# First attention of a gated cross-attention kernel: an own PSUM tile for greatest scores, sums of two key tiles together, small products for both token tiles, shorter roots, and a new opening

## The chip, the cores and the metric

The kernel runs on one core of a Trainium2 chip. The metric is the device time of one execution in microseconds. One execution was also profiled; durations, waits and the clock granted to TensorE come from it. PE is TensorE's matmul, PEld its weight load, DVE is VectorE, ACT is ScalarE, POOL is GpSimd, SP is SyncE, which issues most DMAs.

## The reference, cut to what matters

Two layers, each of cross attention and a feed-forward part, on 4 batches of 256 tokens of width 256 and a context of 1601 tokens of width 128. The change lies in the cross attention of the first layer alone:

```python
y_dca = y[:, -DCA:, :]          # the last 16 context tokens
y_main = y[:, :-DCA, :]         # 1585 others
k_dca = _ln(kv_dca[:, :, 0], kn_dca_w, kn_dca_b)
q = _ln((x @ Wq + bq).reshape(b, s1, H, HD), qn_w, qn_b)
kv = jnp.concatenate([y_main @ Wk + bk, y_main @ Wv + bv], axis=-1)
kv = kv.reshape(b, s2, H, 2 * HD)
k = _ln(kv[..., :HD], kn_w, kn_b)          # per head of 16
v = kv[..., HD:]
ctx = _attn(qT, k.transpose(0, 2, 1, 3), v.transpose(0, 2, 1, 3))
ctx_dca = _attn(qT, k_dca..., v_dca...)    # a softmax of its own
return (ctx + DCA_WEIGHT * ctx_dca) @ Wo + bo
```

There are 16 heads of width 16; all is fp32. x is layer-normed before, and the result is added to x times the tanh of a gate.

## The kernel before

**Tiling.** The stage handles slabs: a slab is four heads of one batch, so there are 4 x 4 = 16. A head occupies 32 partitions (its width of 16, shared between two slabs), so a product with keys uses 32 rows of the array, and two heads run beside each other in two of its four row groups. The 1585 keys are 13 key tiles of 128, taken in seven pairs, the last a single one. A slab has 14 slots: seven pairs times two halves of its heads.

**A slot.** Each slot emits, in this order:

- A, `attend_tile` (L723 to L742): scores of two heads for two key tiles, four products of 256 columns on 32 rows (L732) into a PSUM tile of two banks, and later their exponential on ACT into `e` (L742).
- G, `greatest_tile` (L676 to L703): for the slab after this one, scores the other way round, two products of 453 columns (L688) into a PSUM tile of two banks, and their maximum on DVE (L697, or L699 for the last columns of both token tiles). The maxima of a slab, 14 G tiles, give its shift (`shift`, L708).
- W, `weigh` (L748 to L766): the sums over one key tile of exponentials times values, four products in four column groups (L757), added up in `ps_o` over the slab.
- What the plan has put into the slot.

The heart of it, and the pools of PSUM tiles:

```python
ps_s = ph.enter_context(tc.tile_pool(name="l0ps_s", bufs=3, space=PSUM))
ps_o = ph.enter_context(tc.tile_pool(name="l0ps_o", bufs=1, space=PSUM))
ps_m = ph.enter_context(tc.tile_pool(name="l0ps_m", bufs=1, space=PSUM))
...
exponentials = attend_tile(u, k)
if ahead:
    v, _ = ahead.pop(0)
    next_greatest(v, 2 - TILES[k][2])
exponentials()
t = k - 2
if t >= 0:
    weigh(u, t)
elif t == -2 and u > 0:
    weigh(u - 1, NKT - 1)
for step in plan.pop(u * SLOTS + k, []):
    step()
```

A and G take turns in the three tiles of `ps_s`. The order on each engine is the order of emission (`keep_order`).

**The plan.** `place` puts a step into a slot; `book` puts one that needs the single tile of `ps_m` (a small product) into the first slot that has none. Small products are: turns of queries (L664), heads into the token layout (`add_heads`, L779), turned heads and output projection per token tile (L795, L803), layer norms (L130), query projections (L551), key products (L472), root sums (L502), values (L535), the last tokens' attention in four products per token tile (L588, L596, L618, L626), and routing for the later part (L202, L241). The scaling of keys (`key_scale`, L525 and L527) takes a tile of `ps_s`. Batch b + 1 is prepared while batch b is attended.

**Roots.** A key's variance per head comes from a product of its squares with `hsum` (L502), 16 heads and one column for the unscaled last rows on 32 partitions, for four groups of 397 keys; then a logarithm, an exponential and a Newton step on 128 x 397 (L509 to L516), and a product with `sel` that spreads the roots over the heads' rows (L525).

**The opening.** Before the first slot the kernel loads weights and the first context, prepares batch 0 (keys, queries, roots, values), the 16 last keys of all batches (`prepare_last`, L402), makes the 14 G tiles of slab 0 and the first four (`LEAD`) of slab 1.

Of the kernel before, what the change touches and what calls it, by code (L numbers as in the profile page):

```python
# [21 lines left out]
P = 128  # L22
# [10 lines left out]
H = 16  # L33
# [26 lines left out]
def tile_gated_cross_blocks(ctx: ExitStack, tc: tile.TileContext, a: dict, out: bass.AP):  # L60
# [49 lines left out]
    def layernorm_steps(b, pst, tag="ps_t"):  # L110
# [15 lines left out]
        yield  # L126
        for i, xn in enumerate(xns):
            pt = pst.tile([P, 512], F32, name=tag)
            for c in range(DC):
                nc.tensor.transpose(pt[:, c * P : (c + 1) * P], xn[:, c * P : (c + 1) * P], ident)  # L130
            nc.scalar.copy(
                xnT[b][:, :, i * P : (i + 1) * P],
                pt[:, : DC * P].rearrange("p (c t) -> p c t", c=DC),
            )
            yield
# [126 lines left out]
    KG = (NMAIN + NG - 1) // NG  # L262
# [4 lines left out]
    with ExitStack() as ph:  # L267
# [7 lines left out]
        ps_s = ph.enter_context(tc.tile_pool(name="l0ps_s", bufs=3, space=PSUM))  # L275
# [17 lines left out]
        wkv = wp.tile([P, 2 * D], F32, name="wkv")  # L293
# [3 lines left out]
        for i, n in enumerate(("L0_xattn_bk", "L0_xattn_bv")):  # L297
# [9 lines left out]
        hn = {  # L307
            n: bcast_row(wp, f"L0_xattn_{n}", HD0, nc.sync if "dca" in n else nc.scalar)
            for n in ("qn_w", "qn_b", "kn_b", "kn_w", "kn_dca_w", "kn_dca_b")
        }  # L310
        NB = B * DCA
        cd = lp.tile([P, NB], F32, name="cd")
        nc.sync.dma_start(out=cd.rearrange("p (b k) -> p b k", b=B), in_=a["ctxT"][:, :, NMAIN:])
        wdca = load(lp, "wdca", [P, 2 * D], a["Wkv_dca"])
        bdca = bcast_row(lp, "bkv_dca", 2 * D)
        bkv = lp.tile([NB, 2 * D], F32, name="bkv")
        for i, n in enumerate(("L0_xattn_bk", "L0_xattn_bv")):
            nc.sync.dma_start(out=bkv[:, i * D : (i + 1) * D], in_=a[n].partition_broadcast(NB))
        load_gates()
        for t in range(QT, 2 * QT):  # L320
            load_x(t)
        for g in range(NG):
            load_context(1, g)
        wo = load(wp, "wo0", [P, DC, D], a["L0_xattn_Wo"].rearrange("(c p) n -> p c n", p=P))
        bo = bcast_row(wp, "L0_xattn_bo", D)
        for t in range(2 * QT, NT):
            load_x(t)
# [6 lines left out]
        epsc = wp.tile([P, 1], F32, name="epsc")  # L334
        hsum = wp.tile([P, 2, W], F32, name="hsum")
        hsel = wp.tile([P, 2, NG, W], F32, name="hsel")
        sel = wp.tile([P, 2, P], F32, name="sel0")
# [14 lines left out]
        for c in range(2):  # L352
            nc.gpsimd.tensor_scalar(hsum[:, c, c * HW : (c + 1) * HW], bmask, 1.0 / HD0, None, ALU.mult)
# [3 lines left out]
        for c in range(2):  # L357
            nc.gpsimd.tensor_copy(hsel[:, c, :, c * HW : (c + 1) * HW], bc_mid(last_row, NG))
            nc.gpsimd.tensor_copy(hsel[:, c, :, H], m15.to_broadcast([P, NG]))
# [17 lines left out]
        w4, b4 = (x.rearrange("p (c h e) -> p c h e", c=2, e=2 * HD0) for x in (wkv, brow))  # L377
# [24 lines left out]
        def prepare_last():  # L402

            rep = lp.tile([NB, B, HG, DCA], F32, name="rep", bufs=1)
# [6 lines left out]
            kd = lp.tile([P, H, HD0], F32, name="kd", bufs=1)  # L411
            vd = lp.tile([P, H, HD0], F32, name="vd", bufs=1)
            ph3, bd3, bm3 = (x.rearrange("p (h e) -> p h e", e=2 * HD0) for x in (pm[:NB], bdca[:NB], bkv))
            nc.vector.tensor_tensor(kd[:NB], ph3[:, :, :HD0], bd3[:, :, :HD0], ALU.add)
            nc.vector.tensor_tensor(vd[:NB], ph3[:, :, HD0:], bd3[:, :, HD0:], ALU.add)

            nc.gpsimd.tensor_tensor(vd[:NB], vd[:NB], bm3[:, :, HD0:], ALU.add)
            yield
            center(kd[:NB], kd[:NB])
            sqd = lp.tile([P, H, HD0], F32, name="sqd", bufs=1)  # L420
            nc.scalar.activation(sqd[:NB], kd[:NB], AF.Square)
            yield
            v, y, t = (lp.tile([NB, H], F32, name=f"d_{k}", bufs=1) for k in "vyt")
            nc.vector.reduce_sum(v, sqd[:NB], axis=AX.X)
# [4 lines left out]
            nc.gpsimd.tensor_tensor(kd[:NB], kd[:NB], bc_last(v, HD0), ALU.mult)  # L429
            nc.gpsimd.tensor_tensor(kd[:NB], kd[:NB], bc_mid(hn["kn_dca_w"][:NB], H), ALU.mult)  # L430
            nc.gpsimd.tensor_tensor(kd[:NB], kd[:NB], bc_mid(hn["kn_dca_b"][:NB], H), ALU.add)
            yield
            pt = ps_m.tile([P, 512], F32, name="ps_m")
            for c in range(DC):
                nc.tensor.transpose(
                    pt[:, c * NB : (c + 1) * NB],
                    kd[:NB, c * HG : (c + 1) * HG, :].rearrange("p h d -> p (h d)"),
                    ident[:NB, :NB],
                )
            kdT = lp.tile([P, DC, NB], F32, name="kdT", bufs=1)  # L440
# [7 lines left out]
            for b in range(0, B, 2):  # L448
                pv = ps_m.tile([P, 512], F32, name="ps_m")
                for k in range(2):  # L450
# [3 lines left out]
                        rhs=vd[:NB].rearrange("p h d -> p (h d)"),  # L454
                        start=True,
                        stop=True,
                    )
                for k in range(2):
                    for c in range(DC):
                        nc.vector.tensor_tensor(  # L460
                            vdb[b + k][:, c],
                            pv[:, k * D + c * P : k * D + (c + 1) * P].rearrange("p (h d) -> p h d", d=HD0),
                            bc_last(bmask, HD0),
                            ALU.mult,
                        )
                yield

# [27 lines left out]
        def key_roots(b):  # L495

            v, y, t = (hp.tile([P, KG], F32, name=f"r_{k}") for k in "vyt")
            roots[b] = v
            pm = ps_m.tile([P, 512], F32, name="ps_m")
            for c in range(2):  # L500
                for g in range(NG):
                    nc.tensor.matmul(  # L502
                        pm[g * W : (g + 1) * W, :KG],
                        lhsT=hsum[:, c],
                        rhs=sq[:, c, g * KG : (g + 1) * KG],
                        start=c == 0,
                        stop=c == 1,
                    )
            nc.vector.tensor_scalar(v, pm[:, :KG], epsc, None, ALU.add)  # L509
# [9 lines left out]
        def key_scale(b, c, half):  # L519

            ps = ps_s.tile([P, 2, 512], F32, name="ps_s")
            for i in range(2):
                g = 2 * half + i
                rows = slice(g * W, (g + 1) * W)
                nc.tensor.matmul(ps[:, i, :KG], lhsT=sel[rows, c], rhs=roots[b][rows], start=True, stop=True)  # L525
            k3 = kTs[b % 2][:, c, 2 * half * KG : 2 * (half + 1) * KG].rearrange("p (i k) -> p i k", i=2)
            nc.vector.tensor_tensor(k3, k3, ps[:, :, :KG], ALU.mult)  # L527
# [18 lines left out]
        aos = [[fix.tile([P, D], F32, name=f"ao{j}{i}") for i in range(QT)] for j in range(2)]  # L546

        def query_project(b, i):
            pm = ps_m.tile([P, 512], F32, name="ps_m")
            for c in range(DC):  # L550
                nc.tensor.matmul(  # L551
                    pm[:, :D], lhsT=xnT[b][:, c, i * P : (i + 1) * P], rhs=wq[:, c, :], start=c == 0, stop=c == DC - 1
                )
            nc.vector.tensor_tensor(qraw[:, i].rearrange("p h d -> p (h d)"), pm[:, :D], bq, ALU.add)

        def query_steps(b, eng):
# [18 lines left out]

            eng.tensor_tensor(sqq, q3, bc_mid(hn["kn_b"], QT * H), ALU.mult)
            yield
            nc.vector.reduce_sum(qcs[b % 2].rearrange("p i h -> p (i h)"), sqq, axis=AX.X)
            eng.tensor_tensor(kb, q3, bc_mid(hn["kn_w"], QT * H), ALU.mult)
            yield  # L580

        def last_tokens(b):

            qn = qraw
# [1071 lines left out]
```

## Time and profile before

| | us |
|---|---|
| median of three runs | 1623.56 (1615.42 to 1623.99) |
| the profiled execution: its own time | 1621.13 |
| its span, first to last instruction | 1619.4 |
| opening of the stage, to the first A | 77.1 |
| the 224 slots | 500.3 |
| later stages | 1042 |

The rows of the profile name engine, line and operation, then what it writes from what it reads. A busy PE includes waits between its row groups, so PE's share of 97% does not say that the array is full. In a timeline row the first number is the start, the second the length; what stands in brackets is the idle time of the engine before it and what ended it. In the rows by stretches of time, busy time and number of instructions stand by engine, then the granted clock, the share of the DMA engines and the traffic.

### The profile page before, as it was taken

The page shows a single profiled execution, that of the slowest core. Times are in us where ns is not written, and L with a number is a line of the kernel's source. Part 1 is how long each engine was busy: PE and PEld are TensorE (multiplying, and loading weights), DVE is VectorE, ACT ScalarE, POOL GpSimd, SP SyncE. Part 2 cuts the span into 40 slices and gives each one's busy share as a digit, 9 for nine tenths or more (in the row PEclk, how much of TensorE's full clock was granted, in tenths as well). Part 3 has the DMA queues.
Part 4 walks back from the last instruction along what each step waited for, and adds up shares of the span by engine and source line. Part 5 has one row for each costly group of instructions (what it writes and reads, how often), then busy time and mean ns, then how long its engine had stood idle before and what let it go on. Part 6 is the DMA issues. An engine that isn't in the chain of part 4 may idle for free.

```text
span 1619.4 us, 31284 instructions
## 1 busy us (share of the span) xinstructions
PE 1566.6 (97%) x12200; PEld 915.5 (57%) x12200; DVE 1100.0 (68%) x2409; ACT 795.3 (49%) x1837; POOL 514.2 (32%) x424
## 2 busy tenths in 40 slices
PE   4899999999999999989999999999999999999998
PEld 2454544554555545446666666666666666666665
DVE  5566576566567436677777777777877778777655
ACT  2256556556555534444445454554445444454443
POOL 1101001001001124434445444454444444444410
PEclk8689999999999999989999999999999999999999
DMA  4000000000010040000000000000000000000000
GB/s 123 21 1 1 21 1 1 1 2 10 1 49 15 14 179 1 1 2 8 9 15 15 15 9 16 8 22 3 15 9 15 21 9 15 9 2 2 2 1 27
DMA packets 44713, 28.06 MB, mean 17 GB/s; under 512 B 29586, under 2 KB 40212, under 8 KB 44436
## 3 DMA queue, kind: packets, MB, share of 16 engines
q1 hardware_dynamic: 30852, 24.82, 5.3%
q10 hardware_dynamic: 13712, 1.23, 0.6%
q8 instruction: 96, 1.57, 0.4%
q14 instruction: 53, 0.43, 0.1%
HBM read 24.18 MB, written 1.05 MB: 16 GB/s over the span
## 4 chain that ended last, share of the span: by engine, by line
PE 88%; DVE 4%; ACT 3%; issue 3%; POOL 1%; DMA 1%; ACTq 0%; SPq 0%; DVEq 0%; POOLq 0%
PE ps_o L1433 21%; PE ps_sc L1370 20%; PE ps_s L732 9%; PE ps_o L757 7%; PE ps_s L688 7%; PE ps_y L1451 4%; PE ps_m L1359 3%; PE ps_v L1193 2%; PE ps_m L535 2%; PE ps_m L472 1%; ACT pr L1385 1%; PE ps_a L1207 1%; PE ps_m L664 1%; DVE mxs L697 1%; PE ps_g L1564 1%
## 5 line engine op out<-in xcount | busy, mean ns | idle before, releaser
L1420 POOL TENSOR_TENSOR pr<-pr,rs 128x1604 f32<-128x1604 f32 x128 | 364.0, 2865 | 432.4 <-DMA rs<-ws 386.2
L1433 PE MATMUL ps_o<-pT,cx 128*128 128x256 f32 x1664 | 372.5, 381 | 8.3 <-DVE pT L1426 8.3
L1370 PE MATMUL ps_sc<-ctxT,qT 128*32 128x401 f32 x4096 | 359.5, 502 | 0.5 <-DVE nm L1377 0.5
L1377 DVE CUSTOM_DVE_ANT_0 pr<-ps_sc,mk 128x401 f32<-128x401 f32 x512 | 294.1, 576 | 93.7 <-PE ps_sc L1370 55.3
L1385 ACT ACTIVATE pr<-pr,nm 128x401 f32<-128x401 f32 x512 | 320.8, 628 | 70.1 <-DVE nm L1377 69.6
L1433 PEld LDWEIGHTS ps_o<-pT,cx 128*128 128x128 f32 x1664 | 317.9, 191 | 53.1 <-DVE pT L1426 9.4
L697 DVE TENSOR_REDUCE mxs<-ps_s 128x2 f32<-128x906 f32 x192 | 210.4, 1100 | 139.7 <-PE ps_s L732 70.0
L742 ACT ACTIVATE e<-ps_s 128x1024 f32<-128x1024 f32 (+1 forms) x224 | 215.2, 963 | 174.8 <-PE ps_s L732 156.3
L1426 DVE STREAM_TRANSPOSE pT<-pr 128x1664 f32<-128x1664 f32 x128 | 242.9, 1899 | 4.9 <-POOL pr L1420 4.9
L1370 PEld LDWEIGHTS ps_sc<-ctxT,qT 128*32 128x32 f32 x4096 | 126.3, 110 | 204.3 <-issue 119.7
L732 PE MATMUL ps_s<-qT,kT 32*128 32x256 f32 x1664 | 240.1, 405 | 1.0 <-ACT e L742 0.9
L688 PE MATMUL ps_s<-kT,qT 32*128 32x453 f32 (+1 forms) x1024 | 232.3, 563 | 2.1 <-ACT e L742 1.2
L732 PEld LDWEIGHTS ps_s<-qT,kT 32*128 32x128 f32 x1664 | 142.2, 186 | 73.1 <-issue 39.7
L757 PE MATMUL ps_o<-e,vp 128*32 128x256 f32 x1664 | 134.3, 392 | 0.6 <-ACT e L742 0.6
L1402 ACT ACTIVATE ws<-ws 32x32 f32<-32x32 f32 x64 | 14.6, 228 | 194.1 <-DVE ws L1401 194.1
L1443 ACT COPY ao<-ps_o 128x256 f32<-128x256 f32 x64 | 23.8, 372 | 153.5 <-PE ps_o L1433 130.2
L1385 ACT ACTIVATION_READ_ACCUMULATOR pr<-pr,nm 128x1 f32 x512 | 95.5, 187 | 0.0
L688 PEld LDWEIGHTS ps_s<-kT,qT 32*128 32x128 f32 x1024 | 80.1, 192 | 11.7 <-issue 3.8
L757 PEld LDWEIGHTS ps_o<-e,vp 128*32 128x32 f32 x1664 | 33.2, 108 | 91.0 <-issue 88.5
L788 POOL TENSOR_TENSOR ao<-ao,on 128x64 f32<-128x64 f32 x32 | 10.4, 326 | 228.5 <-DVE rs L783 168.2
L1451 PE MATMUL ps_y<-vo,ao 128*128 128x256 f32 x256 | 72.3, 405 | 0.1
L1451 PEld LDWEIGHTS ps_y<-vo,ao 128*128 128x128 f32 x256 | 43.3, 189 | 44.5 <-ACT pr L1385 39.9
(291 smaller groups left out, 1505.8 us busy)
## 6 DMA issues: line engine op xcount, KB each, us to landing
ctxT<-in_ctxT_dram SPq DMA_DIRECT2D x4, 800.5 KB, 10.8
ctx<-in_ctxT_dram SPq DMA_DIRECT2D x12, 198.5 KB, 3.5
kT<-in_L_xattn_Wq_dram SPq DMA_DIRECT2D x4, 512.0 KB, 3.6
wo<-in_L_xattn_Wo_dram SPq DMA_DIRECT2D x4, 512.0 KB, 5.4
bq<-nm SPq DMA_DIRECT2D x128, 2.0 KB, 1.7
bq<-nm ACTq DMA_DIRECT2D x128, 2.0 KB, 2.0
rs<-ws SPq DMA_DIRECT2D x128, 1.0 KB, 1.9
rs<-ws ACTq DMA_DIRECT2D x128, 1.0 KB, 1.7
```

Source lines behind the costliest of these rows:

```text
L688: nc.tensor.matmul(ps[:, k, m * w : (m + 1) * w], lhsT=qT[rows, ii * P : (ii + 1) * P], rhs=kT[rows, s // 2, n * CW0 : n * CW0 + w], start ...
L697: nc.vector.tensor_reduce(mx[:, i, r : r + 2, n], ps[:, :, :w], AX.X, ALU.max)
L732: nc.tensor.matmul(ps[:, k, jj * S : (jj + 1) * S], lhsT=kT[rows, s // 2, (j + jj) * P : (j + jj + 1) * P], rhs=qT[rows], start=True, stop ...
L742: nc.scalar.activation(e[:, :, : nj * S], ps[:, :, : nj * S], AF.Exp)
L757: nc.tensor.matmul(summed[u][(r + k) * W : (r + k + 1) * W, :S], lhsT=vps[b % 2][:, t, h * VW : h * VW + W], rhs=made[u, j, r][:, k, jj * ...
L1370: nc.tensor.matmul(ps[i * TQ : (i + 1) * TQ, :KS], lhsT=queries[u][:, t * TQ : (t + 1) * TQ], rhs=ctxT[b][:, i * KS : (i + 1) * KS], start ...
L1377: nc.vector.tensor_tensor_reduce(out=prs[u % 3][:, t, :KS], in0=ps[:, :KS], in1=masks[b], scale=-1.0, scalar=3.0e38, op0=ALU.add, op1=ALU. ...
L1385: nc.scalar.activation(p, p, AF.Exp, bias=found[u][:, 0, t : t + 1], scale=-1.0, accum_out=found[u][:, 1, t : t + 1])
L1420: nc.gpsimd.tensor_tensor(p, p, bc_last(factors[:, ts], KS), ALU.mult)
L1426: nc.vector.transpose(pTs[u % 2][:, ts].rearrange("p t k -> p (t k)"), prs[u % 3][:, ts].rearrange("p t k -> p (t k)"))
L1433: nc.tensor.matmul(po[:, u % 2], lhsT=contexts[b][:, k, :], rhs=pTs[u % 2].rearrange("p t (k q) -> p t k q", q=TQ)[:, :, k, :], start=k == ...
L1451: nc.tensor.matmul(ys[b][:, i], lhsT=outs[u][:, i * P : (i + 1) * P], rhs=vo[:, h, :], start=(h, i) == (0, 0), stop=(h, i) == (H - 1, QT - 1),
```

## The change

- **PSUM.** `ps_s` has two tiles instead of three and is A's; a new pool `ps_g` with one tile is G's. In the opening, where there is no A, G and the first keys rotate over all three.
- **W.** In even slots W handles the two key tiles whose A tiles were made in the two slots before, together; in odd slots there is none. Slot 0 of a slab holds the last key tile of the slab before, alone.
- **Small products** for both token tiles in one group: transposes of tokens, query projection, the last tokens' four products, turned heads, output projection. `book` uses odd slots only; keys, values, roots and the last tokens may use any.
- **Roots** on 128 x 199: each group of 397 keys is halved, the halves lie in the two halves of the 32 partitions; root sums and spreading take twice as many products of half the columns. The unscaled row is added in `key_scale` by DVE (`m15`) instead of by a column of `sel`.
- **Opening.** `prepare_last` and the last tokens of batch 0 move into the first slots; slab 1's first four G tiles move into slots 1, 2, 5 and 6 of slab 0 (`CATCH_UP`). Most loads are issued after the first weights are centred (`load_rest`); the second key weights share the tile of the first (`w_first`). Three values are made while the roots are computed. The copies of `prepare_last` go to ACT and its arithmetic, with the output's gating, to POOL.

```diff
-        ps_s = ph.enter_context(tc.tile_pool(name="l0ps_s", bufs=3, space=PSUM))
+        ps_s = ph.enter_context(tc.tile_pool(name="l0ps_s", bufs=2, space=PSUM))
+        ps_g = ph.enter_context(tc.tile_pool(name="l0ps_g", bufs=1, space=PSUM))
...
-        def greatest_tile(u, n, i, r):
+        def greatest_tile(u, n, i, r, pool=None):
...
-            ps = ps_s.tile([P, 2, 512], F32, name="ps_s")
+            ps = (pool or ps_g).tile([P, 2, 512], F32, name="ps_g" if pool is None else "ps_s")
...
-        def book(slot, step):
+        def book(slot, step, any_slot=False):
...
-            while slot in taken:
+            while slot in taken or not (any_slot or slot % 2):
                 slot += 1
...
+        CATCH_UP = {1: 2, 2: 0, 5: 2, 6: 0}
...
-        for k in range(HALF_SLAB):
-            next_greatest(0, 0)
-            next_greatest(0, 2)
-            value_project(0, next(values))
-            next(last0, None)
...
+        for k in range(2 * HALF_SLAB):
+            next_greatest(0, k % 2 * 2, (ps_s, ps_s, None)[k % 3])
+            if k == 3:
+                for _ in qs0:
+                    pass
+            if k % 3 == 2:
+                value_project(0, next(values))
...
         turn_queries(0, 1)
-        turn_queries(1, 0)
-        for k in range(LEAD):
-            next_greatest(1, (2, 0)[k % 2])
-        for _ in last0:
-            pass
...
                 if ahead:
-                    v, _ = ahead.pop(0)
-                    next_greatest(v, 2 - TILES[k][2])
+                    next_greatest(ahead.pop(0), 2 - TILES[k][2])
                 exponentials()
-                t = k - 2
-                if t >= 0:
-                    weigh(u, t)
-                elif t == -2 and u > 0:
-                    weigh(u - 1, NKT - 1)
+                if u == 0 and k in CATCH_UP:
+                    next_greatest(ahead.pop(0), CATCH_UP[k])
+                if k % 2 == 0:
+                    for t in (k - 2, k - 1):
+                        if t >= 0:
+                            weigh(u, t)
+                    if k == 0 and u > 0:
+                        weigh(u - 1, NKT - 1)
```

The roots and one of the merged products:

```diff
-            v, y, t = (hp.tile([P, KG], F32, name=f"r_{k}") for k in "vyt")
+            v, y, t = (hp.tile([P, KH], F32, name=f"r_{k}") for k in "vyt")
...
-        def query_project(b, i):
-            pm = ps_m.tile([P, 512], F32, name="ps_m")
-            for c in range(DC):
-                nc.tensor.matmul(
-                    pm[:, :D], lhsT=xnT[b][:, c, i * P : (i + 1) * P], rhs=wq[:, c, :], start=c == 0, stop=c == DC - 1
-                )
+        def query_project(b):
+            pm = ps_m.tile([P, QT, D], F32, name="ps_m")
+            for i in range(QT):
+                for c in range(DC):
+                    nc.tensor.matmul(
+                        pm[:, i], lhsT=xnT[b][:, c, i * P : (i + 1) * P], rhs=wq[:, c, :], start=c == 0, stop=c == DC - 1
+                    )
...
-            nc.vector.tensor_tensor(k3, k3, ps[:, :, :KG], ALU.mult)
+            nc.vector.scalar_tensor_tensor(k3, ps[:, :, :KG], m15, k3, ALU.add, ALU.mult)
```

The order in which the changed opening prepares batch 0:

```diff
+        wdca, wo, bo = load_rest()
+        next(ln0)
...
         first_keys(2)
-        for i in range(QT):
-            query_project(0, i)
+        query_project(0)
+        first_keys(3)
         next(qs0)
...
+        values = iter(VALUES)
+        for k in range(3):
+            value_project(0, next(values))
...
+        key_scale(0, 0, 0)
         stage_queries(0)
+        stage_queries(1)
         turn_queries(0, 0)
-        stage_queries(1)
+        key_scale(0, 0, 1, ps_g)
+        turn_queries(1, 0)
```

## The prediction

> **What bounds the kernel now.** I read the page first, for the whole, then the busy time and clock by stretches, to see which stage the change lies in, and then the timeline of two slots, because only there one sees what an instruction waits for.
>
> ```profile
> span 1619.4 us, 31284 instructions
> PE 1566.6 (97%) x12200; PEld 915.5 (57%) x12200; DVE 1100.0 (68%) x2409; ACT 795.3 (49%) x1837; POOL 514.2 (32%) x424
> ...
> L697 DVE TENSOR_REDUCE mxs<-ps_s 128x2 f32<-128x906 f32 x192 | 210.4, 1100 | 139.7 <-PE ps_s L732 70.0
> L742 ACT ACTIVATE e<-ps_s 128x1024 f32<-128x1024 f32 (+1 forms) x224 | 215.2, 963 | 174.8 <-PE ps_s L732 156.3
> ```
>
> TensorE is busy 97% of the span. The reduction of a G tile takes 1.10 us, the exponential of an A tile about 1.02.
>
> ```profile
> 0.00:77.00 77.00, 49.80 (x182) 23.27 (x184) 43.59 (x93) 19.88 (x39) 14.43 (x58) 0.75 0.26 76
> 77.00:577.00 500.00, 493.45 (x4784) 254.96 (x4782) 305.21 (x488) 287.24 (x407) 53.72 (x106) 0.99 0.04 11
> ...
> 25.00:30.00 5.00, 0.86 (x8) 0.52 (x8) 3.77 (x7) 0.62 (x2) 0.00 (x0) 0.77 0.00 0
> 50.00:55.00 5.00, 3.12 (x15) 1.74 (x16) 4.79 (x9) 3.79 (x6) 1.83 (x3) 1.00 0.00 2
> 55.00:60.00 5.00, 4.23 (x16) 1.94 (x15) 1.15 (x2) 0.85 (x2) 2.84 (x9) 0.50 0.00 0
> 85.00:90.00 5.00, 5.00 (x42) 2.65 (x34) 2.12 (x4) 1.25 (x2) 0.00 (x0) 0.58 0.00 0
> ```
>
> These rows give stretch, length, then busy time (and instructions) of PE, PEld, DVE, ACT, POOL, then the granted clock. The stage has an opening of 77 us with much idle PE and half clock in most of it from 27 us on, and a loop of 224 slots from 77.1 to 577.4 (500.3 us, 2.23 a slot), where PE always has something in hand. Slabs 0 to 14, which carry a G tile in each slot but the last four, take 478.8 us; slab 15 takes 21.5.
>
> ```profile
> 303.44 0.48 PE L732 MATMUL ps_s<-qT,kT 32*128 32x256 f32 x2
> 303.46 0.65 PE L688 MATMUL ps_s<-kT,qT 32*128 32x453 f32 x2
> ...
> 304.50 0.64 PE L757 MATMUL ps_o<-e,vp 128*32 128x256 f32 x8
> 304.68 1.03 ACT L742 ACTIVATE e<-ps_s 128x1024 f32<-128x1024 f32 x1 [0.55 <-PE ps_s L732]
> 304.68 1.10 DVE L697 TENSOR_REDUCE mxs<-ps_s 128x2 f32<-128x906 f32 x1 [1.59 <-PE ps_s L732]
> ...
> 305.07 0.44 PE L664 MATMUL ps_m<-ident,qp 128*128 128x128 f32 x2
> ...
> 305.44 0.48 PE L732 MATMUL ps_s<-qT,kT 32*128 32x256 f32 x2
> ...
> 305.76 0.64 PE L688 MATMUL ps_s<-kT,qT 32*128 32x453 f32 x1
> ...
> 306.24 0.55 PE L688 MATMUL ps_s<-kT,qT 32*128 32x453 f32 x2
> ...
> 306.71 0.64 PE L757 MATMUL ps_o<-e,vp 128*32 128x256 f32 x8
> 306.83 1.10 DVE L697 TENSOR_REDUCE mxs<-ps_s 128x2 f32<-128x906 f32 x1 [1.05 <-PE ps_s L688]
> ```
>
> Read the starts. A and G run side by side in different row groups, 1.06 us together (303.44 to 304.50); W takes 0.57 (to 305.07); a turn of queries 0.37 (to 305.44). The next G starts only at 305.76: its buffer is freed when the exponential of 304.68 ends at 305.71. W behind it starts at 306.71, not 306.50: PE keeps its order, and a G that waits holds all behind it. So already now PE's busy time hides waits: two slots with a turn of queries take 2.00 and 2.22.
>
> **The change, part by part.**
>
> *G's own tile.* G gets one PSUM tile for itself, so the next G waits for the reduction of this one. All four terms are in the rows: G 1.03 us (305.76 to 306.79), 0.04 to the reduction (306.83), 1.10, and 0.05 from a freed buffer to the next G (305.71 to 305.76): 2.23 us from G to G, whatever PE does. Today the ring of three lets G follow at 1.99 to 2.29 in such slots; the mean from G to G over the loop is 2.28, but that includes the slots where PE itself needs longer. There are 206 such slots in slabs 0 to 14: 206 x 2.23 = 459.4. Queued behind a waiting G: its own slot's W and small product, and the next A. Who waits for those is ACT and DVE, neither of which is full.
>
> *Sums of two key tiles together.* A change between row groups and column groups costs: W streams two rounds of 0.216 (the rounds of A start 0.216 apart), 0.43, and takes 0.57. Two together are not in the trace: at least 4 x 0.216 = 0.86, at most 2 x 0.57 = 1.14; by the row, 0.57 + 0.43 = 1.00. They saved 0.14 here and about 0.1 where A follows A, some 20 us over the loop if PE set the pace. But G sets it: an even slot without small product needs 0.96 (G to W) + 1.00 + 0.03 = 1.99 of PE, an odd one 0.99 + its small product, both under 2.23.
>
> *Small products, and where they lie.* Where PE's path is over 2.23, the excess counts. Laying the plan of the diff out slot by slot gives 52 even slots that have W and a small product. Their prices, from rows of before: key product 0.87 (a slot of 2.50 beside 1.63), value product 1.06 (302.38 to 303.44), root sums 1.56, scaling 0.77, four transposes 0.6, four products of the last tokens 1.08. So 1.99 + 0.87 = 2.86 and 0.63 over for a key, 0.82 for a value, and so on: 36 us for the 52. Odd slots hold three query and three output projections, now for both token tiles: 1.06 + 4 x 0.216 = 1.92, 0.68 over each, and with a root sum 5 us; slots 0 of a slab 1 us: together 42. After such a slot A and G start together and the reduction waits for both (1.22 after G's start in the first row, not 1.07): 0.14 x 58 = 8 us. The merging itself removes nine groups a batch, each 0.15 of switching, which I count inside these prices.
>
> *Four tiles caught up.* The opening no longer makes four G tiles of slab 1; slots 1, 2, 5 and 6 make two each. The second waits for the first with all of PE behind it: 4 x 2.23 = 8.9. The last four slots of slab 14 then have no G: 7.0.
>
> *Shorter roots.* DVE and ACT steps on 199 instead of 397 columns: 0.57 to about 0.3 each. In the loop they lie beside PE: nothing; without that cover four batches x 6 steps x 0.27 = 6 us gained. In the opening they count.
>
> *Work on other engines.* Output gating and the last keys' steps go to POOL (32% busy); they are awaited slots later. If their cover went: at most 2 us at slot 5, where the transposes follow 2.0 us of POOL. DVE per slot, 1.42 us in the loop, fits into 2.23; pairs of 0.68 for the last tokens push a reduction by 0.3, four times. I take nothing, and 6 us for the upper end.
>
> *The opening.* Before, the first G starts at 36.4, then 18 reductions share PE with seven value products and the preparation of the last keys until 77.1. After: the first keys wait for the transposes of the selection, whose copy sits behind ACT's DMA issues (it started at 9.81), then for four bias products of 1.19: about +1 us. The roots save 0.25 + 0.5 + 0.8, one scaling (0.98) and the products with kn_b (1.37) move behind the first G: first reduction at about 33.7 instead of 38.3. From there 14 reductions x 1.10 + 1.4 for the moved DVE pair + 1.2 for shift and turn: A starts at 52. The 21 DMA issues that now follow the wait for the weight tile go out from SP some 4 us later (10.5 instead of 6.4); gates, tokens and context of batch 1 are read after 50 us, and the second layer's weights behind them on SP far later. Gain 25. If the clock is halved while G runs (a G 1.9, a value 2.08), it is 10 less; if nothing of the start is delayed and the gaps close, 6 more.
>
> *The clock, rule and row.* The Trainium skill, TensorE: Matmul & The Clock Gate, "Part 1", ties half clock to an idle window of about 3.4 us. By that the new loop, reached without such a gap, would start at full clock. The rows disagree: half clock from 55 on, although PE was busy 3.12 of the 5 us before, and back only at 89. I follow the rows: some 12 us of the loop at half clock again, a G then 1.9, and as fewer G fit in: 4 us.
>
> *One buffer or two, rule and row.* The same page, "HAM oscillation", reports that double-buffering PSUM gave a dense kernel no further gain. By it G's single tile would be free and the loop PE's alone: 421 us for the 15 slabs by the prices above, plus catching up, a gain of over 70 in all. The row shows the opposite wait already (305.44 to 305.76, for a buffer); I follow the row.
>
> **Sum**, against the profiled execution's own 1621.1 us (span 1619.4 and 1.7 around it; 2.4 under the median of the runs, 1623.6). Slabs 0 to 14: 459.4 + 42 + 8 + 8.9 + 7.0 + 4 = 529.3, for 478.8: +50.5. Slab 15, no G, bound by W and the exponential: 20.5 for 21.5: -1. Opening: -25. End of the stage, two groups fewer: -0.6. Together +23.9: 1645.
>
> **The rivals.** *Faster: PE sets the pace.* If G to G took less than PE's path, the pairing of W and the fewer groups would come through. The place is the odd slot's G. By the same laying out the loop balances the opening's gain when the link is 2.05 us; below that the change wins: at 1.9 the 15 slabs come to about 487 and the whole to 1621 + 8 - 26.6 = 1603, with no link at all to about 433 and 1549. For it: the plan puts W or a small product between any two G. Against it: four durations in the trace that sum to 2.23, none of which the change touches. I give 0.10 to a result over 0.5% faster.
> *The clock stays down.* The G phase and slab 0 at half clock: G to G 1.9 + 0.04 + 1.10 + 0.05 = 3.1. Opening 10 longer, 14 slots instead of four at +0.9 another 9: 1664. For it: 55 to 89 at half clock. Against it: the three value products now fill the gap of 25 to 30. 0.17.
> *Evenly matched.* The excess is half of mine, because A runs ahead and W pairs cost less, and the opening ends at 48: 1645 - 20 - 4 = 1621; close to the point of no change. 0.15.
> My own case has 0.58.
>
> **How the numbers follow.** Half a per cent, 8 us, is about what a measurement of this kernel can tell from no change. My case with its bounds (opening 46 to 58, excess 30 to 50, DVE 0 to 6) spans 1631 to 1660. The range for 8 in 10 takes in most of the clock case and of the even case: 1622 to 1666. Faster 0.10, same 0.15, slower 0.75 (my case and the clock case).
>
> **What would show it.** Right: the first A near 52; G's weights waiting for DVE's reductions (that group of waits now has 2 us, three times) in more than half the slots; slabs 13 and 14 at 31 to 32 us each though they hold few small products; W groups of about 1.00. Wrong: G starting before the last reduction ended; slabs 12 to 14 shorter than their 30.4, 28.8 and 26.3 of now; an opening under 40.

## The result, and the profile after

The changed kernel took 1664.56 us (median of four runs, 1663.15 to 1670.43) against 1619.67 for the kernel before, measured beside it: ratio 1.0284, interval 1.0239 to 1.0329. It is slower by 2.8%. The profiled execution took 1665.64, 44.5 more than the profiled one of before; the forecast sum had been +23.9.

Page of the changed kernel, its head and four groups (line, engine, operation, tiles, count; then busy time and mean ns of one; then idle time of the engine before them, and what ended most of it):

```profile
span 1663.8 us, 31418 instructions
PE 1596.4 (96%) x12330; PEld 951.1 (57%) x12330; DVE 1085.4 (65%) x2328; ACT 790.9 (48%) x1811; POOL 531.1 (32%) x433
...
L732 DVE TENSOR_REDUCE mxs<-ps_g 128x2 f32<-128x906 f32 x184 | 202.7, 1102 | 183.0 <-PE ps_g L723 106.0
...
L723 PE MATMUL ps_g<-kT,qT 32*128 32x453 f32 (+1 forms) x976 | 229.7, 557 | 15.3 <-DVE mxs L732 14.6
...
L792 PE MATMUL ps_o<-e,vp 128*32 128x256 f32 x1664 | 120.5, 395 | 3.0 <-ACT e L777 3.0
...
L723 PEld LDWEIGHTS ps_g<-kT,qT 32*128 32x128 f32 x976 | 78.8, 190 | 39.5 <-DVE mxs L732 36.6
```

And two groups of the kernel before:

```profile
L757 PE MATMUL ps_o<-e,vp 128*32 128x256 f32 x1664 | 134.3, 392 | 0.6 <-ACT e L742 0.6
L688 PEld LDWEIGHTS ps_s<-kT,qT 32*128 32x128 f32 x1024 | 80.1, 192 | 11.7 <-issue 3.8 <-ACT e L742 2.4 <-DVE mxs L697 2.0
```

G's weights (last row of the changed kernel) now stand idle 36.6 us for the reduction; before, it was 2.0. Counted in the timeline, the first product of G starts within 0.12 us of the end of a reduction in 130 of the 192 slots of slabs 1 to 14 that have a G; before, in 8. The sums (L792) are busy for 120.5 us, where they were 134.3: the pairing did save its switches, and DVE has less to do than before. PE is busy for 30 us more all the same: 26 of them lie in slabs 1 to 14, where a wait between its row groups counts as busy, and 18 in slab 0, where the clock was halved; the opening has 12 less.

Busy time by stretches of the changed kernel: opening, slab 0, slabs 1 to 14, slab 15 (stretch, length, PE, PEld, DVE, ACT, POOL, then the granted clock):

```profile
0.00:55.10 55.10, 37.41 (x180) 19.67 (x180) 35.37 (x65) 17.71 (x32) 9.99 (x48) 0.96 0.35 103
55.10:115.90 60.80, 53.38 (x330) 27.10 (x331) 27.97 (x41) 18.96 (x27) 12.82 (x27) 0.64 0.00 1
115.90:598.20 482.30, 463.62 (x4385) 257.93 (x4384) 270.68 (x397) 252.57 (x346) 55.43 (x93) 1.00 0.03 9
598.20:620.60 22.40, 19.60 (x214) 9.80 (x214) 0.50 (x2) 13.45 (x16) 2.41 (x2) 1.00 0.23 72
```

And the kernel before, cut at the same places:

```profile
0.00:77.10 77.10, 49.90 (x182) 23.27 (x184) 43.69 (x93) 19.88 (x39) 14.43 (x58) 0.75 0.26 76
77.10:112.30 35.20, 34.99 (x303) 18.68 (x299) 23.50 (x36) 16.59 (x23) 2.36 (x5) 0.83 0.01 2
112.30:555.90 443.60, 437.86 (x4283) 225.86 (x4282) 280.90 (x449) 257.40 (x370) 48.72 (x98) 1.00 0.04 9
555.90:577.40 21.50, 20.90 (x210) 10.49 (x210) 0.72 (x4) 13.26 (x15) 2.64 (x3) 1.00 0.21 73
```

By places: opening -22.0, slab 0 +25.6, slabs 1 to 14 +38.7, slab 15 +0.9, after the stage +1.2; together +44.4, the difference of the spans. Slabs 1 to 14 run at full clock in both kernels, so their loss is none of the clock; slab 0 has a granted clock of 0.64. The loop's times repeat well (slab 4 took 39.07 to 39.08 in four runs with the same loop); the opening and slab 0 are single executions in which the clock came and went.

The link itself, in two plain slots of slab 2 (timeline of the changed kernel: start, length, engine, line, operation, then in brackets the idle time before it):

```profile
162.87 0.65 PE L723 MATMUL ps_g<-kT,qT 32*128 32x453 f32 x2
...
163.83 1.07 PE L792 MATMUL ps_o<-e,vp 128*32 128x256 f32 x16
163.94 1.10 DVE L732 TENSOR_REDUCE mxs<-ps_g 128x2 f32<-128x906 f32 x1 [0.18 <-PE ps_g L723]
...
164.83 0.48 PE L767 MATMUL ps_s<-qT,kT 32*128 32x256 f32 x2
165.10 0.65 PE L723 MATMUL ps_g<-kT,qT 32*128 32x453 f32 x2
```

From G to G 162.87 to 165.10: 2.23 us. A starts at 164.83, as soon as the pair of sums is through; G behind it has to wait until the reduction of 163.94 ends at 165.04. The sums of a pair take 1.00 (163.83 to 164.83). Both are the numbers of the forecast. In slabs 1 to 14 no two G start less than 2.23 apart; before, the least was 1.54.

### The profile page after: what moved, and what is told of

Read it like the earlier page. It is cut to its first block, busy times and chain, and to the rows that moved or that the text cites. A ratio compares the mean times of both kernels' runs of the same rounds, so it can differ in the third digit from the quotient of the medians.

```text
span 1663.8 us, 31418 instructions
## 1 busy us (share of the span) xinstructions
PE 1596.4 (96%) x12330; PEld 951.1 (57%) x12330; DVE 1085.4 (65%) x2328; ACT 790.9 (48%) x1811; POOL 531.1 (32%) x433
## 4 chain that ended last, share of the span: by engine, by line
PE 83%; DVE 7%; ACT 4%; issue 3%; POOL 1%; DMA 1%; ACTq 0%; SPq 0%; DVEq 0%; POOLq 0%
PE ps_o L1458 20%; PE ps_sc L1395 20%; PE ps_s L767 8%; PE ps_g L723 7%; PE ps_o L792 6%; PE ps_y L1476 4%; PE ps_m L1384 3%; DVE mxs L732 3%; PE ps_v L1218 2%; PE ps_m L554 1%; ACT pr L1410 1%; PE ps_a L1232 1%; PE ps_m L486 1%; ACT kT L490 1%; ACT kT L497 1%
## 5 line engine op out<-in xcount | busy, mean ns | idle before, releaser
L1410 ACT ACTIVATE pr<-pr,nm 128x401 f32<-128x401 f32 x512 | 321.0, 628 | 68.1 <-DVE nm L1402 66.9
L732 DVE TENSOR_REDUCE mxs<-ps_g 128x2 f32<-128x906 f32 x184 | 202.7, 1102 | 183.0 <-PE ps_g L723 106.0
L723 PE MATMUL ps_g<-kT,qT 32*128 32x453 f32 (+1 forms) x976 | 229.7, 557 | 15.3 <-DVE mxs L732 14.6
L792 PE MATMUL ps_o<-e,vp 128*32 128x256 f32 x1664 | 120.5, 395 | 3.0 <-ACT e L777 3.0
L723 PEld LDWEIGHTS ps_g<-kT,qT 32*128 32x128 f32 x976 | 78.8, 190 | 39.5 <-DVE mxs L732 36.6
L792 PEld LDWEIGHTS ps_o<-e,vp 128*32 128x32 f32 x1664 | 44.3, 111 | 84.5 <-issue 62.6
L1476 PEld LDWEIGHTS ps_y<-vo,ao 128*128 128x128 f32 x256 | 43.4, 189 | 44.4 <-ACT pr L1410 39.9
L1384 PE MATMUL ps_m<-xnT,aq 128*128 128x256 f32 x256 | 65.8, 380 | 0.0
```

Of the source, the lines that this page charges most:

```text
L723: nc.tensor.matmul(ps[:, k, m * w : (m + 1) * w], lhsT=qT[rows, ii * P : (ii + 1) * P], rhs=kT[rows, s // 2, n * CW0 : n * CW0 + w], start ...
L732: nc.vector.tensor_reduce(mx[:, i, r : r + 2, n], ps[:, :, :w], AX.X, ALU.max)
L792: nc.tensor.matmul(summed[u][(r + k) * W : (r + k + 1) * W, :S], lhsT=vps[b % 2][:, t, h * VW : h * VW + W], rhs=made[u, j, r][:, k, jj * ...
L1410: nc.scalar.activation(p, p, AF.Exp, bias=found[u][:, 0, t : t + 1], scale=-1.0, accum_out=found[u][:, 1, t : t + 1])
L1476: nc.tensor.matmul(ys[b][:, i], lhsT=outs[u][:, i * P : (i + 1) * P], rhs=vo[:, h, :], start=(h, i) == (0, 0), stop=(h, i) == (H - 1, QT - 1),
```

## The experiments

Times of slabs are from the starts of A in each trace. The kernel before ran beside each group.

**The ring of three again.** From the changed kernel:

```diff
-        ps_s = ph.enter_context(tc.tile_pool(name="l0ps_s", bufs=2, space=PSUM))
-        ps_g = ph.enter_context(tc.tile_pool(name="l0ps_g", bufs=1, space=PSUM))
+        ps_s = ph.enter_context(tc.tile_pool(name="l0ps_s", bufs=3, space=PSUM))
...
-            ps = (pool or ps_g).tile([P, 2, 512], F32, name="ps_g" if pool is None else "ps_s")
+            ps = ps_s.tile([P, 2, 512], F32, name="ps_s")
```

> The changed kernel, with one thing undone: the tile of greatest scores (G) has no PSUM tile of its own, A, G and the key products share a ring of three two-bank tiles again. Theory (the own single tile sets the slot, 2.23 us from one G to the next): slabs 1 to 14 fall from 482 us together to 452-465, because G then waits for an exp of three tiles back and the slot is bound by the exps at about 2.1; the slots with the single-tile sum stay. Total 1635 to 1650. Rival (the pairing of the sums, with uneven slots of small products, costs the loop, and the tile of its own does not): slabs 1 to 14 stay above 473, total above 1655.

Measured: 1625.96 us, ratio to before 1.0046 (1.0029 to 1.0062). Slabs 1 to 14 take 457.5 instead of 482.3, slab 0 takes 48.1 instead of 60.8. The loop is as the theory has it, and the total lies under the expected 1635 to 1650, because slab 0, which the expectation left out, gained too: the own tile costs 24.8 us in the 14 slabs and 12.7 more in slab 0, most of the loss. Against the kernel before 13.9 us stay lost in the 14 slabs, so there is a second cause.

**The own tile alone.** From the kernel before:

```diff
-        ps_s = ph.enter_context(tc.tile_pool(name="l0ps_s", bufs=3, space=PSUM))
+        ps_s = ph.enter_context(tc.tile_pool(name="l0ps_s", bufs=2, space=PSUM))
+        ps_g = ph.enter_context(tc.tile_pool(name="l0ps_g", bufs=1, space=PSUM))
...
-            ps = ps_s.tile([P, 2, 512], F32, name="ps_s")
+            ps = ps_g.tile([P, 2, 512], F32, name="ps_g")
```

> The kernel before, with the own single PSUM tile for the tile of greatest scores alone (two tiles left for the others), nothing else of the change. Theory: in slots whose other work fits under 2.23 us the link binds, the slots with small products were longer than 2.23 already and G waits for no more there; slabs 0 to 14 rise from 478.8 to 490-500, total 1630 to 1642. Rival (the own tile alone is free, the loss needs the pairing): total within 4 us of the kernel before.

Measured: 1677.12, ratio 1.0361 (1.0338 to 1.0384), slower even than the whole change. Slabs 0 to 14 take 504.3, 25.5 more than before and a little over what was expected. What was not expected is the opening: first A at 107.3 instead of 77.1, with the clock at a half from 28 to 120:

```profile
50.00:70.00 20.00, 16.38 (x38) 6.24 (x36) 8.40 (x14) 5.17 (x9) 2.04 (x3) 0.50 0.00 1
70.00:90.00 20.00, 16.15 (x44) 7.73 (x44) 5.80 (x9) 1.44 (x3) 3.93 (x13) 0.50 0.00 0
```

There all G tiles of the opening go through the one tile, and at half clock a link takes 3.1 instead of 2.23. (The changed kernel avoids this in its opening: its G tiles use all three buffers there.) The rival, that the own tile is free without the pairing, falls.

**The four tiles back in the opening.** From the changed kernel:

```diff
+        for k in range(2):
+            next_greatest(1, (2, 0)[k], (None, ps_s)[k])
...
+        for k in range(2, LEAD):
+            next_greatest(1, (2, 0)[k % 2], (ps_s, None)[k % 2])
...
-                if u == 0 and k in CATCH_UP:
-                    next_greatest(ahead.pop(0), CATCH_UP[k])
```

> The changed kernel, with the four tiles of greatest scores of slab 1 issued in the opening again, and not caught up in slots of slab 0. Theory (the caught-up tiles, met by a half clock, cost slab 0): first A 3 to 6 us later (58 to 61 for 55.1), slab 0 of 40 to 46 us for 60.8, total 1650 to 1656. Rival (slab 0 is long because the clock is at half there whatever is placed in it): slab 0 stays above 52, total 1662 or more.

Measured: 1656.24, ratio 1.0230 (1.0207 to 1.0254). First A at 59.3, slab 0 takes 41.3 instead of 60.8: both as expected; the total is at the upper edge of what was. The profiled execution also had a stretch of half clock from 282 to 292, which added 4 us to slab 6. Half clock after the opening lasted until 66.9 only, against 105 with the tiles caught up. So the four tiles cost 19.5 us in slab 0 where they save 4.2 in the opening; how much of the 19.5 is the tiles and how much the longer half clock, this run does not separate.

**Two one-bank tiles for G,** one for each head, each with a reduction of its own. From the changed kernel:

```diff
+                ps = [ps_g.tile([P, 512], F32, name="ps_g") for _ in range(2)]
...
-                nc.vector.tensor_reduce(mx[:, i, r : r + 2, n], ps[:, :, :w], AX.X, ALU.max)
+                for k in range(2):
+                    nc.vector.tensor_reduce(mx[:, i, r + k, n : n + 1], ps[k][:, :w], AX.X, ALU.max)
```

> The changed kernel, with the own two-bank tile of G split into two one-bank tiles, each with its own reduction over 453 columns (twice as many reductions, half as long). Theory (the slot is the chain of G's products and one reduction over the whole tile): G of one head may refill while the other head is reduced, the link falls from 2.23 to about 1.75, PE sets the pace, slabs 1 to 14 take 400 to 425 for 482, total 1580 to 1605, under the kernel before. Rival (the vector engine or the exps bind close behind): slabs 1 to 14 stay above 450, total above 1630.

Measured: 1658.37, ratio 1.0235 (1.0205 to 1.0266); slabs 1 to 14 take 482.4, the same as in the changed kernel, though some 5 of them come from two stretches of half clock in this execution (472.5 to 479.3 and 537.3 to 544.2). This expectation failed. The timeline of a plain slot of slab 7 shows where the time went:

```profile
341.66 1.17 DVE L737 TENSOR_REDUCE mxs<-ps_g 128x1 f32<-128x453 f32 x2 [1.08 <-PE ps_g L727]
...
342.34 0.29 PEld L727 LDWEIGHTS ps_g<-kT,qT 32*128 32x128 f32 x2 [0.23 <-DVE mxs L737]
342.35 1.56 PE L727 MATMUL ps_g<-kT,qT 32*128 32x453 f32 x4
342.88 0.29 PEld L727 LDWEIGHTS ps_g<-kT,qT 32*128 32x128 f32 x2 [0.24 <-DVE mxs L737]
...
343.83 1.07 PE L796 MATMUL ps_o<-e,vp 128*32 128x256 f32 x16
```

The first head's products start after the first reduction (342.34), as hoped, and the link does fall, from 340.46 to 342.35: 1.89. But the second head's products wait for the second reduction (342.88), and PE keeps its order. G takes 1.48 to the sums instead of 0.96, and the sums start half a microsecond later. The wait was moved into G, not removed. So this run speaks neither for nor against the theory of the link; the next one on the reduction does.

**Half the reduction.** The changed kernel, with the maximum of a whole tile taken over half of its columns:

```diff
-                nc.vector.tensor_reduce(mx[:, i, r : r + 2, n], ps[:, :, :w], AX.X, ALU.max)
+                nc.vector.tensor_reduce(mx[:, i, r : r + 2, n], ps[:, :, : w // 2], AX.X, ALU.max)
```

> The changed kernel, but DVE takes the maximum of a whole tile of G over the first half of its columns only (226 of 453 a head; the other half is left out of the shift), so that a reduction takes about 0.58 instead of 1.10. Theory (the slot is the chain G, reduction, G): the link falls to about 1.7, slabs 1 to 14 fall from 482 to 420-440, total 1595 to 1615. Rival (something else, the exps of A's two tiles or PE, holds the slot at 2.1 or more whatever the reduction takes; the split into two tiles moved nothing): slabs 1 to 14 stay above 455.

Measured: 1610.21, ratio to before 0.9944 (0.9919 to 0.9970). Slabs 1 to 14 take 444.3, 38.0 less than in the changed kernel, a little above the range. One duration on DVE, which is 65% busy over the span, is worth 38 us of the loop; the rival, that something else holds the slot, falls. A shorter link also let the opening end at 50.7 and slab 0 at 45.8.

```profile
L732 DVE TENSOR_REDUCE mxs<-ps_g 128x2 f32<-128x452 f32 x184 | 115.7, 629 | 208.0 <-PE ps_s L767 136.3
```

The reduction takes 0.63. In slots where A and G start together it begins 1.21 after G and not 1.07, so the link is 1.75 to 1.9; that is why the gain is short of the 42 us and more that were expected.

**Ring of three and the four tiles in the opening,** the first and the third edit together.

> The changed kernel with the ring of three tiles for A and G and with the four tiles of slab 1 in the opening again; sums in pairs and the new opening stay. Theory (the two losses are separate places): slabs 1 to 14 as with the ring alone, 457; slab 0 falls from 48.1 to 37-41, first A at 57-61; total 1616 to 1624, level with the kernel before. Rival (the two undoings gain the same microseconds, both being the waits of slab 0): total stays at 1624 to 1630.

Measured: 1623.82 (20 runs), ratio 1.0026 (1.0012 to 1.0041). Slabs 1 to 14: 457.6 again. Slab 0: 42.5 instead of 48.1, a little over what was expected; first A at 60.5, 5.2 later. The gain of the second edit is 2 us here, where it was 8 beside the own tile: with a ring, caught-up tiles cost little more than tiles in the opening. The theory of two separate losses holds for slabs 1 to 14 only; in slab 0 they are largely the same microseconds.

**Single sums again.** As the last one, and besides:

```diff
-                if k % 2 == 0:
-                    for t in (k - 2, k - 1):
-                        if t >= 0:
-                            weigh(u, t)
-                    if k == 0 and u > 0:
-                        weigh(u - 1, NKT - 1)
+                t = k - 2
+                if t >= 0:
+                    weigh(u, t)
+                elif t == -2 and u > 0:
+                    weigh(u - 1, NKT - 1)
...
-        def book(slot, step, any_slot=False):
+        def book(slot, step, any_slot=True):
```

> As the ring of three with the four tiles in the opening, and besides one key tile's sum in each slot again and small products in any slot, as before the change; what is left of the change is the new opening, the merged small products and the shorter roots. Theory (pairs make even slots too long, up to 2.9 with a small product, and odd ones short, and a ring of three cannot carry time from one to the other): slabs 1 to 14 fall from 457 to 435-448, total 1596 to 1612, faster than the kernel before. Rival (pairs save their 0.14 us a slot and cost nothing; single sums add 14 us): slabs 1 to 14 at 457 or more, total above 1618.

Measured: 1600.47, ratio to before 0.9881 (0.9847 to 0.9915): faster than both kernels. Slabs 1 to 14 take 438.9. Its stretches and three groups:

```profile
57.10:96.70 39.60, 37.03 (x322) 18.88 (x318) 25.82 (x39) 18.48 (x26) 12.77 (x27) 0.86 0.01 2
96.70:535.60 438.90, 437.73 (x4384) 234.35 (x4383) 273.20 (x396) 256.49 (x349) 55.35 (x93) 1.00 0.04 10
...
L722 PE MATMUL ps_s<-kT,qT 32*128 32x453 f32 (+1 forms) x1024 | 228.9, 542 | 0.6 <-ACT e L776 0.3
L791 PE MATMUL ps_o<-e,vp 128*32 128x256 f32 x1664 | 134.0, 393 | 0.0
L722 PEld LDWEIGHTS ps_s<-kT,qT 32*128 32x128 f32 x1024 | 79.5, 185 | 8.4 <-DVE mxs L731 4.2
```

The sums are back at 134.0 us of busy time, 15 more than with pairs and the ring (119.1), and yet the 14 slabs are 18.7 us shorter. Slab 7, a short one, shows both: with pairs its even slots take 2.1 to 3.4 and its odd ones 0.9 to 2.2, 29.2 together; with single sums most slots are of 1.63 and of 2.2 to 2.7 in turn, 28.0 together. That the uneven slots are the cause fits this, but no run shows it by itself. The edit has two parts, the sums and the slots that `book` may use; they were not tried apart, so "the pairs" below means both.

**The fourth corner: own tile with single sums,** the last edit on the changed kernel with the four tiles in the opening.

> As the version with single sums, small products in any slot and the four tiles in the opening, but with the changed kernel's own single tile for G: the fourth corner of tile (ring or own) by sums (single or paired). Theory (the own tile's link of 2.23 binds whatever the sums are): slabs 1 to 14 at 462-470 for 438.9 with the ring, total 1622 to 1636; the own tile costs 23 to 31 us here, about as much as with pairs (24.8). Rival (the own tile costs only because the pairs leave odd slots short): slabs 1 to 14 under 452, total under 1615.

Measured: 1634.09, ratio 1.0082 (1.0055 to 1.0109); slabs 1 to 14 take 470.5. The own tile costs 31.6 us here, just above what was expected. The four corners of slabs 1 to 14:

| us | ring of three | own tile for G | own tile costs |
|---|---|---|---|
| sums in pairs, small products mostly in odd slots | 457.5 | 482.3 | 24.8 |
| single sums, any slot | 438.9 | 470.5 | 31.6 |
| kernel before (single, a group per token tile) | 443.6 | 466.5 | 22.9 |

Each part costs by itself, and the columns add up to the loss: 24.8 for the own tile and 18.6 for the pairs, less the 4.7 that the rest of the change gains there (438.9 for 443.6, with merged small products and shorter roots), make 38.7. The two are not independent: beside the own tile the pairs cost 11.8 (482.3 for 470.5), beside the ring 18.6.

**The clock of slab 0: the gap filled.** The changed kernel with four products of 128 rows and 400 columns where PE idles from 51.3 to 54.1:

```diff
+        pm = ps_m.tile([P, 512], F32, name="ps_m")
+        for _ in range(4):
+            nc.tensor.matmul(pm[:, :400], lhsT=ident, rhs=sq[:, 0, :400], start=True, stop=True)
```

> The changed kernel, with four products on all 128 rows (400 columns, not used) put on PE between the last product of the opening and the turn of the queries, where PE idles from 51.3 to 54.0. Theory (the idle window takes the clock to a half, and slab 0 is long for it): the clock stays full past 61, slab 0 falls from 60.8 to 46-50, total 1648 to 1656. Rival (the clock falls in slab 0 whatever PE did in those 3 us): half clock for over 20 us of slab 0 again, slab 0 above 55, total within 5 us of the changed kernel.

Measured: 1663.10, ratio 1.0265 (1.0235 to 1.0296), the changed kernel's time. The clock fell at 61.2 instead of 54.2, and was then at a half for nearly all the time to 102:

```profile
54.00:61.20 7.20, 4.89 (x40) 2.38 (x40) 2.92 (x3) 3.56 (x5) 2.13 (x3) 1.00 0.01 2
61.20:102.20 41.00, 36.49 (x206) 18.48 (x206) 17.70 (x28) 10.11 (x15) 9.62 (x23) 0.54 0.00 1
```

Slab 0 took 58.3. The gap sets when the clock falls, perhaps, but not whether it stays down. The rival holds.

**The clock of slab 0: the slots filled.** The changed kernel with one such product between A and G in each slot of slab 0:

```diff
+                if u == 0:
+                    pm = ps_m.tile([P, 512], F32, name="ps_m")
+                    nc.tensor.matmul(pm[:, :400], lhsT=ident, rhs=sel_columns, start=True, stop=True)
```

(`sel_columns` stands for the first 400 columns of `sel`.)

> The changed kernel with one more product on all 128 rows (400 columns, its result not used) between A and G in each slot of slab 0, where PE waits for DVE; it is to fill the waits while the clock is at a half. Theory (the clock stays down because PE waits in its slots, and comes back once it is filled): full clock by 85 for 105, slab 0 between 50 and 60 although it has 14 products more. Rival (the clock's return does not follow from how PE is filled): half clock until past 95, slab 0 at 62 or more, total 1665 to 1675.

Measured: 1707.23, ratio 1.0527 (1.0490 to 1.0565), far beyond both expectations. The clock was at a half from 58.9 to 147.6 but for 3.4 us, and slab 0 took 100.8. Between 62 and 148 PE stood idle four times, 1.2 us each:

```profile
80.00:85.00 5.00, 5.00 (x26) 2.25 (x28) 1.10 (x1) 0.00 (x0) 0.00 (x0) 0.50 0.00 0
120.00:125.00 5.00, 5.00 (x16) 1.97 (x14) 1.10 (x1) 0.70 (x2) 0.00 (x0) 0.50 0.00 0
```

The theory that PE's idle time keeps the clock down falls: filled, the clock stayed down longer. But the product also parted A from G, so that the two no longer ran side by side; six of the slab's 14 slots took 6.1 to 7.3. So this is no clean price of the product, and PE, though busy, did less in a given time (see the last section).

## Why the prediction was right, and which of its sizes were off

The direction, the main mechanism and its place were right: a link of 2.23 us that the change sets by G's single tile, worth more than the opening gains. The measured median lies 20 us above the forecast and 1.4 inside the range, which had been drawn that wide for the case of a lasting half clock; one of the four runs, 1670.43, lies outside. So the mechanism was right; that the number still fell into the range is in part luck.

- *G's own tile.* Predicted 2.23 from four durations; measured 2.23. G waits for the reduction in 130 of 192 slots. Right, and shown by three pairs of runs with and without it, and by the halved reduction.
- *Small products in even slots, 36 of the 42 us over the link.* By the plan's prices slabs 1 to 14 come to about 481 of the 529.3 (the rest is slab 0: 14 x 2.23, 8.9, 4 and some 4 of its own excess); measured 482.3. It is not spread evenly: slabs 4 and 8 took 39.1, slabs 7, 11, 12 and 13 32.1 each, against 31.2 for 14 links. The ring's corner shows that the pairs cost by themselves, 18.6 us, and not only as an addition to the link.
- *Sums of two key tiles, 1.00.* Measured 1.00. The 14 us they save in busy time brought nothing, as said.
- *The opening, -25.* Measured -22.0, but not by the forecast's path. The first G starts at 36.4 in both kernels: the shorter roots and what was moved behind them brought, in sum, nothing up to there, and the first reduction came at 37.5 and not 33.7, 0.8 earlier than before only because G ran at full clock. The gain lies behind it, from the first reduction to the first A: 17.6 us for 38.8.
- *The last slots.* Slab 15 +0.9 for -1, the end +1.2 for -0.6: small, but 3.7 us together.
- *The signs.* First A at 55.1 for 52, slab 13 at 32.1, as named. Slab 14 took 28.7, under the 31 to 32 named; its last four slots have no G, and by the forecast's own terms it comes to 10 x 2.23 + 7.0 = 29.3.
- *Four tiles caught up, 8.9, and the clock, 4.* This is the step that was mis-sized: 13 us for what came out in slab 0 as some 26. By these terms slab 0 is about 48; it took 60.8, and that is 13 of the 20.5 us between the forecast sum and the profile (the opening has 3 more, the last slots and the end 3.7). Half clock lasted to 105 with short returns, not for 12 us of the loop, and there the link takes 3.1: 1.88 for G, 1.10 for the reduction, and the handovers:

```profile
64.61 1.88 PE L723 MATMUL ps_g<-kT,qT 32*128 32x453 f32 x4 [1.09 <-DVE mxs L732]
66.54 1.10 DVE L732 TENSOR_REDUCE mxs<-ps_g 128x2 f32<-128x906 f32 x1 [1.47 <-PE ps_g L723]
67.69 1.88 PE L723 MATMUL ps_g<-kT,qT 32*128 32x453 f32 x4 [1.20 <-DVE mxs L732]
69.50 1.94 PE L792 MATMUL ps_o<-e,vp 128*32 128x256 f32 x16
```

In this slot 2 of slab 0 (8.98 us) two links of 3.1 stand one behind the other, and the sums, which had nothing to wait for, start at 69.50 behind them all.

Of the rivals, *the clock stays down* gave 1664, the time that came, but by its sum only in part: the opening was at full clock (0.96), so its 10 us did not come; its 9 us in slab 0 did, and some 4 more. That it met the time is chance. *PE sets the pace* is refuted by the reductions. Its crossing was sized fairly: it put a link of 1.9 at 487 for the 15 slabs and 1603 in all; the halved reduction, with a link of 1.75 to 1.9, took 490 and 1610.

Rule and row: the row was right to be followed on buffers. The rule of the Trainium skill on the clock, in TensorE: Matmul & The Clock Gate, "Part 1", would have a PE that is kept busy return to full clock after one window. If busy means the profile's busy time, the run with filled slots contradicts it in this stage; by the work done in a window (last section) the traces come close to it.

## What to carry to other kernels

Before a PSUM tile is set aside for one producer, add fill, drain and the two handovers, and compare the sum with the slot: a single tile makes it the least time of the slot, whatever the engines' shares say. Work that is merged to save switches is not gained until the slots show it: where buffers tie slots together, pairs of sums saved 15 us of PE's busy time here and the loop was 18.7 us longer. Splitting a tile so that part of it comes free sooner helps only if what goes into the second part is not queued directly behind the first on an engine that keeps its order.

## What the runs showed of the hardware

A half clock came in every kernel around the end of its opening, from 10 us (four tiles in the opening) to 92 (the own tile alone, 28 to 120). At half clock a link took 3.1 instead of 2.23.

The traces show more than the experiments asked for. In all twelve the clock changes only on a grid of 3.41 us, in the changed kernel at 54.2, 61.0, 64.4, 78.1, 81.5 and 105.4. Cut at this grid, the attention stages (from 14 us to the last exponential) have 2044 windows. PE's busy time does not tell what the clock does next: of 104 windows at half clock in which PE was busy throughout, 65 were followed by another at half. What PE did in the window tells nearly always. Take for each matmul record the time that its columns need at full clock (0.216 us for 256 columns in fp32), times the share of the 128 x 128 array that it uses (a quarter for A, G and W), and add this up over the window, as a share of it. Of 156 windows under 0.36, 146 were followed by half clock; of 1858 from 0.40 on, all were followed by full clock; in between, 15 of 30. Four windows of the changed kernel and two of the run with filled slots:

| window from, us | clock | PE busy | work | clock after it |
|---|---|---|---|---|
| changed, 95.1 | half | 1.00 | 0.35 | half |
| 98.6 | half | 1.00 | 0.31 | half |
| 102.0 | half | 1.00 | 0.39 | full |
| 105.4 | full | 1.00 | 0.81 | full |
| filled slots, 86.2 | half | 1.00 | 0.28 | half |
| 89.6 | half | 1.00 | 0.29 | half |

So a half clock tends to hold itself, because it halves what PE can do in a window. By the same reckoning G or A alone, two products beside each other, comes to 0.25 at most at half clock, and only A and G together, or W with its four, come to 0.5: the product that parted A from G lowered the work although it filled the waits. In slabs 1 to 14 of the changed kernel the work is 0.375 or more in every window, and the clock stays full although PE waits. This was read from finished traces; no run was made to test it, and eight of the ten windows that break it stand between 52 and 64 us, where slab 0 begins.
